# Offsets of two snake convolutions moved ahead of the last product series of a 9x9 convolution

## The chip, the cores and the metric

The kernel runs on one core of a Trainium2 chip. Its time is the time of the device in microseconds (us). A core has a matrix engine (TensorE, in the profile PE for the products and PEld for the loading of their stationary operand), a vector engine (VectorE, DVE), an activation engine (ScalarE, ACT), a general engine (GpSimd, POOL) and a synchronising engine (SyncE, SP). Each takes its own instructions strictly in the order in which the program holds them. Transfers (DMAs) are issued by an engine's queue (SPq and ACTq here) and then run beside the engines. SBUF is the on-chip memory of 128 partitions, PSUM the memory into which TensorE writes.

## The reference, cut to what matters

The kernel computes a sequence of four layers on two images of 128 channels and 64x64 pixels: an attention, a block of three convolutions in parallel, a residual step and a state-space scan in four directions. The change lies in the second layer alone:

```python
h = gelu(affine(conv2d(x, cv1_w, 1), cv1_g, cv1_b))             # stem, 3x3, 64 channels
o0 = silu(affine(conv2d(h, conv0_w, K // 2), conv0_g, conv0_b)) # the 9x9 convolution, 128 channels
ox = dsconv(h, ..., morph=0)                                    # snake along one axis
oy = dsconv(h, ..., morph=1)                                    # and along the other
out = silu(affine(conv2d(concatenate([o0, ox, oy]), fuse_w, 0), fuse_g, fuse_b))

def dsconv(x, ...):
    off = tanh(affine(conv2d(x, off_w, 1) + off_b, off_g, off_beta))  # 18 offsets a pixel
    cum = cumulate_from_center(...)          # running sums of 9 of them, outwards from the middle
    ys = hg + cum                            # (or xs = wg + cum)
    feat = bilinear_sample(x, ys, xs)        # positions are clipped to 0 .. 63
    out = einsum('bkhwc,ock->bohw', feat, w) + b
    return silu(group_norm(out, gn_g, gn_b, out.shape[1] // GN_DIV))
```

The snakes and the 9x9 convolution all read h and nothing of each other. Their three results meet in the 1x1 convolution with fuse_w.

## The kernel before, in words

`layer1` calls three functions one after the other: `stem_and_wide`, `offsets`, `snakes`. All three hold their main work in blocks in which the order of the instructions is the order in which the Python code issues them.

**stem_and_wide** first computes h into the tile `hz` (L560). The 9x9 convolution then runs as a fast algorithm with six combined columns per row (the tiles `comb0` to `comb5`, weights in `w9`), over two halves of the image (k = 0 and 1). For each half there are six series of products, in the order x = 1, 2, 3, 4, 0, 5. A series is 27 pairs of matmuls, one of each pair for each image (L600), into two PSUM tiles. PSUM tiles come from a ring of eight, all with the name m. Behind each series DVE and ACT combine the results (L640 to L661), and `fuse` multiplies finished tiles with the 1x1 weights (L608) and copies them to `xa` (L612 on ACT, L614 on DVE). A finished tile is fused behind the next series, so that the tiles s of series 0 are fused behind series 5, and the tiles q of series 5 at the very end, when nothing is left behind which to hide the silu they wait for.

**offsets** has its own pools. It loads its constants by ACT's queue (L677 to L685), after `layer1` has loaded the snakes' weights on the same queue (L482 to L489). For each of four pairs of row blocks it runs a 3x3 convolution of h (L697, 18 matmuls), a tanh on ACT (L705), the running sums as two matmuls (L709), the adding of the pixel grid on DVE (L711) and four clamps into `yt` (L720), two on DVE and two on POOL. The order is convolution k + 1, then the rest of k. At the end two DMAs on SP's queue store `yt` to the DRAM tensor `pos` (L731).

**snakes** walks over 34 chunks of four lines, 17 for each direction. For a chunk it needs its hats: four DMAs on SP's queue (`positions`, L782) read the positions back from `pos`, spread over 64 partitions each, 256 KB a DMA. ACT then takes the distance of each position from the pixel's index (L791), and DVE clamps it to a triangle (L792). `transposed` turns four lines of h by TensorE (L769) and copies them to `lines` on ACT (L770). `sample` multiplies lines with hats (L809) and copies the result to `feat` (L821, L823), and `convolve` (L835, L846) is run behind every second chunk. The loads run three chunks ahead of the samples and the hats two, in four buffers. Ahead of the loop stand the loads of chunks 0 to 2 and then, for chunks 0 and 1, `transposed` and `hat`.

Of the kernel before, what the change touches and what calls it, by code (L numbers as in the profile page):

```python
# [10 lines left out]
F32 = mybir.dt.float32  # L11
# [4 lines left out]
AF = mybir.ActivationFunctionType  # L16
ALU = mybir.AluOpType
AX = mybir.AxisListType
PSUM = bass.MemoryType.PSUM

P = 128
NB = 2
HW = 64
L = HW * HW
BLK = 512
NBLK = L // BLK
RB = BLK // HW
# [3 lines left out]
KC = K9 // 2  # L31
# [30 lines left out]
def img(t):  # L62
    return t.rearrange("p (r w) -> p r w", w=HW)


def vec(g, name):
    i = VI[name]
    return g.vecs[:, i : i + 1]
# [397 lines left out]
def layer1(g, I):  # L466

    nc, tc = g.nc, g.tc
    with ExitStack() as ctx:
        big = ctx.enter_context(tc.tile_pool(name="l1big", bufs=1))
        hz = big.tile([P, H8, H8], F32, name="hz")
        fw = big.tile([P, 3, P], F32, name="fw")
        nc.scalar.dma_start(fw, I["fuseT"])
        stem_and_wide(g, I, hz, fw)
        pp = ctx.enter_context(tc.tile_pool(name="l1p", bufs=1))  # L480
        grp = pp.tile([P, P], F32, name="grp1")
        nc.scalar.dma_start(grp, I["grp_div"])  # L482

        dsc = pp.tile([P, 2, P], F32, name="dsc")
        dsw = pp.tile([P, 2, KC, P], F32, name="dsw")
        for b in range(2):
            half = slice(64 * b, 64 * b + 64)
            nc.scalar.dma_start(dsc[half], I["dscT"][:, :, KC])
            nc.scalar.dma_start(dsw[half], I["dscT"][:, :, b * (KC + 1) : b * (KC + 1) + KC])  # L489

        dr = ctx.enter_context(tc.tile_pool(name="l1dr", bufs=1, space=bass.MemoryType.DRAM))
        pos = dr.tile([64, L], F32, name="pos")
        offsets(g, I, hz, pos)
        with ExitStack() as bctx:
            snakes(g, bctx, hz, pos, dsc, dsw, grp, fw)


def stem_and_wide(g, I, hz, fw):

# [5 lines left out]
    nc, tc = g.nc, g.tc  # L507
    RP = 32
    NF = HW // 4
    NQ = K9 // 3  # L510
    NX = 6
    CR = RP + KC
    with ExitStack() as ctx:
# [1 line left out]
        ps = ctx.enter_context(tc.tile_pool(name="l1ps", bufs=8, space=PSUM))  # L515

        spdq = [[a.tile([P, BLK], F32, name=f"{n}{b}") for n in "spdq"] for b in range(NB)]
        comb = [a.tile([P, NQ, CR, NF], F32, name=f"comb{i}") for i in range(NX)]

        cw = comb[5].rearrange("p q r i -> p (q r i)")[:, : 9 * 64].rearrange("p (t o) -> p t o", o=64)  # L520
        nc.sync.dma_start(cw, I["cv1T"])
# [94 lines left out]
        with tc.manual_schedule():  # L616
# [10 lines left out]
            ready = []  # L627
            for k in range(HW // RP):
                for x in (1, 2, 3, 4, 0, 5):
                    m = [ps.tile([P, BLK], F32, name="m") for b in range(NB)]  # L630
                    for pair in zip(*(product(m[b], x, b, k) for b in range(NB))):
                        for f in pair:
                            f()
                    for job in ready:
# [30 lines left out]
                fuse(*job)  # L665


def offsets(g, I, hz, pos):

    nc, tc = g.nc, g.tc  # L670
    with ExitStack() as ctx:
        a = ctx.enter_context(tc.tile_pool(name="l1o", bufs=1))
        sm = ctx.enter_context(tc.tile_pool(name="l1osm", bufs=2))
        ps = ctx.enter_context(tc.tile_pool(name="l1ops", bufs=2, space=PSUM))

        ow = a.tile([P, 9, 64], F32, name="ow")
        nc.scalar.dma_start(ow, I["offT"])  # L677
        ov = a.tile([P, 3], F32, name="ov")
        cmat = a.tile([P, 64], F32, name="cmat")
        grid = a.tile([P, NBLK // 2, BLK], F32, name="grid")  # L680
        for e in range(2):
            half = slice(64 * e, 64 * e + 64)
            nc.scalar.dma_start(ov[half], I["offv"])
            nc.scalar.dma_start(cmat[half], I["cum"])
            nc.scalar.dma_start(grid[half], I["grid"].rearrange("p (k e x) -> p k e x", e=2, x=BLK)[:, :, e, :])  # L685
        ob = a.tile([P, 1], F32, name="ob")
        nc.vector.scalar_tensor_tensor(ob, ov[:, 0:1], ov[:, 1:2], ov[:, 2:3], ALU.mult, ALU.add)
        yt = a.tile([64, L], F32, name="yt")

        def conv(k):  # L690
            pc = ps.tile([P, BLK], F32, name="pc")
            for t in range(9):
                dy, dx = divmod(t, 3)
                x0 = KC - 1 + dx
                for e in range(2):
                    y0 = (k + e) * RB + KC - 1 + dy
                    nc.tensor.matmul(  # L697
                        pc[64 * e : 64 * e + 64, :], ow[:, t, :], hz[:, y0 : y0 + RB, x0 : x0 + HW],
                        start=(t == 0), stop=(t == 8),
                    )  # L700
            return pc

        def place(k, pc):
            th = sm.tile([P, BLK], F32, name="th")
            nc.scalar.activation(th, pc, AF.Tanh, bias=ob, scale=ov[:, 0:1])  # L705
            pu = ps.tile([P, BLK], F32, name="pu")
            for e in range(2):
                half = slice(64 * e, 64 * e + 64)
                nc.tensor.matmul(pu[half, :], cmat[half, :], th[half, :], start=True, stop=True)  # L709
            y0 = sm.tile([P, BLK], F32, name="y0")  # L710
            nc.vector.tensor_add(y0, pu, grid[:, k // 2, :])  # L711
            for e in range(2):
                r0 = (k + e) * RB
                for di in range(2):
                    out = img(yt[32 * di : 32 * di + 32])
                    if di == 0:
                        out = out.rearrange("p w h -> p h w")
                    src = img(y0[64 * e + 32 * di : 64 * e + 32 * di + 32])
                    eng = nc.gpsimd if e else nc.vector
                    eng.tensor_scalar(out[:, r0 : r0 + RB, :], src, 0.0, HW - 1.0, ALU.max, ALU.min)  # L720

        with tc.manual_schedule():
            last = None
            for k in range(0, NBLK, 2):
                pc = conv(k)
                if last:
                    place(*last)
                last = (k, pc)
            place(*last)
        for di in range(2):  # L730
            nc.sync.dma_start(pos[32 * di : 32 * di + 32], yt[32 * di : 32 * di + 32])  # L731


def snakes(g, ctx, hz, pos, dsc, dsw, grp, fw):

    nc, tc = g.nc, g.tc
    CN = 4
    NT = KC
    FAR = KC + 1
    NCH = (HW + NT - 1 + CN - 1) // CN  # L740
    RING = 16
    sm = ctx.enter_context(tc.tile_pool(name="l1sm", bufs=2))
    om = ctx.enter_context(tc.tile_pool(name="l1om", bufs=3))
    bp = ctx.enter_context(tc.tile_pool(name="l1b", bufs=1))
    wk = ctx.enter_context(tc.tile_pool(name="l1wk", bufs=4))
    psb = ctx.enter_context(tc.tile_pool(name="l1psb", bufs=2, space=PSUM))
    psf = ctx.enter_context(tc.tile_pool(name="l1psf", bufs=4, space=PSUM))
    psa = ctx.enter_context(tc.tile_pool(name="l1psa", bufs=1, space=PSUM))

    lines = bp.tile([P, RING // CN, CN, 64], F32, name="lines")  # L750

    feat = bp.tile([P, NB, RING, NT, HW], F32, name="feat")
    oraw = bp.tile([P, NB, L], F32, name="oraw")
    hats = {}
# [2 lines left out]

    def transposed(di, n):

        if di > 1 or n >= HW // CN:  # L760
            return
        pt = psb.tile([P, BLK], F32, name="pb")
        v = pt[:, : CN * 64].rearrange("p (i c) -> p i c", c=64)
        for i in range(CN):
            u = n * CN + i + KC
            for b in range(NB):
                half = slice(64 * b, 64 * b + 64)
                line = hz[half, KC : KC + HW, u] if di == 0 else hz[half, u, KC : KC + HW]
                nc.tensor.matmul(v[half, i, :], line, g.ident[half, half], start=True, stop=True)  # L769
        nc.scalar.mul(lines[:, n % (RING // CN)], v, -1.0)  # L770

    def positions(di, m):

        if di > 1:
            return
        hats[di, m] = wk.tile([P, 2, NT, CN, HW], F32, name="hats")
        for b in range(NB):
            for x in range(2):

                o = (32 * di + 9 * b + FAR * x) * L + m * CN * HW  # L780
                src = pos.rearrange("r x -> (r x)")[o : o + NT * (L - HW)].rearrange("(t x) -> t x", x=L - HW)
                nc.sync.dma_start(  # L782
                    hats[di, m][64 * b : 64 * b + 64, x].rearrange("p t i h -> p t (i h)"),
                    src[:, : CN * HW].partition_broadcast(64),
                )

    def hat(di, m):

        if di < 2:
            v = hats[di, m].rearrange("p x t i h -> p (x t i h)")  # L790
            nc.scalar.activation(v, v, AF.Abs, bias=vec(g, "npixel"))  # L791
            nc.vector.tensor_scalar(v, v, 1.0, 0.0, ALU.subtract, ALU.min)  # L792

    def sample(di, m, i):

# [110 lines left out]
        return turns  # L906

    with tc.manual_schedule():
        for n in range(3):
            positions(0, n)  # L910
        for n in range(2):
            transposed(0, n)
            hat(0, n)
        for n in range(2 * NCH):
            di, m = divmod(n, NCH)
            if m == 0:
# [1054 lines left out]
```

## Time and profile before

| what | us |
| --- | --- |
| median of 3 runs (lowest to highest) | 5609.14 (5607.44 to 5610.11) |
| the profiled execution: its time | 5610.11 |
| the profiled execution: its span | 5608.3 |
| start of the first product of the stem (L560) | 1083.1 |
| start of the first product of the 9x9 convolution (L600) | 1146.8 |
| first and last issue of a chunk's load (L782) | 1490.0, 1768.3 |
| first and last start of a sample's product (L809) | 1506.4, 1785.7 |

All times within the kernel count from the start of the profiled span. A line of the timeline or of the chain of waits begins with the start and the duration in us, then comes the engine, then the source line with what it writes and reads, and last, in brackets, how long the engine stood idle before and what it then got. The number behind an x is the number of instructions merged into the line. TensorE makes two passes for a matmul of 32-bit numbers, and the profile counts each: a series of 54 matmuls is x108, a convolution of 18 is x36.

### The profile page before, as it was taken

To read this page: it belongs to the slowest core of one execution; us is meant where nothing else is said; L and a number is where in the kernel's file an instruction comes from. 1 tells how busy PE (TensorE), PEld (TensorE's weight loads), DVE (VectorE), ACT (ScalarE), POOL (GpSimd) and SP (SyncE) were. 2 spreads that over 40 slices of the span, in tenths; PEclk is the share of its full clock that TensorE was granted. 3 is DMA by queue.
4 is the path that set the end of the run, shared out by engine and by line. 5 is a ranking of instruction groups with operands and counts; after the bars stand their busy time and mean duration, and the time that the engine had idled before them with its cause. 6 is when DMAs were issued, how large, how long until landed. Compare 5 with 4: busy or idle time off the path is not lost.

```text
span 5608.3 us, 54471 instructions
## 1 busy us (share of the span) xinstructions
PE 4731.0 (84%) x17062; PEld 1757.8 (31%) x17062; DVE 4537.0 (81%) x4232; ACT 4086.5 (73%) x6282; POOL 3661.7 (65%) x1197
## 2 busy tenths in 40 slices
PE   6999999899788699777788887878888888877786
PEld 3444444344344244222222222222222222222221
DVE  6566555552144998699999999999999999999998
ACT  3999999500255311698888888888888888888886
POOL 6222222100100311599999999999999999999999
PEclk8999999999899899888888888888878787888887
DMA  4111111300375000465565556556555655565554
GB/s 155 38 46 46 31 31 38 62 1 1 76 128 83 27 0 0 104 143 129 129 141 137 135 126 144 129 129 148 140 133 128 144 134 131 130 147 131 134 137 106
DMA packets 334569, 554.27 MB, mean 99 GB/s; under 512 B 69264, under 2 KB 115872, under 8 KB 334080
## 3 DMA queue, kind: packets, MB, share of 16 engines
q1 hardware_dynamic: 331136, 547.17, 41.2%
q10 hardware_dynamic: 3136, 3.56, 0.3%
q8 instruction: 135, 2.21, 0.2%
q14 instruction: 162, 1.33, 0.1%
HBM read 461.40 MB, written 89.13 MB: 98 GB/s over the span
## 4 chain that ended last, share of the span: by engine, by line
DVE 45%; PE 35%; ACT 11%; issue 5%; DMA 2%; POOL 1%; SPq 1%; DVEq 0%; ACTq 0%; POOLq 0%
DVE db L1558 30%; DVE db L1522 11%; PE ps L312 8%; PE acc L328 8%; PE m L1112 5%; PE m L600 5%; ACT da L1544 4%; PE acd L846 2%; ACT db L1550 1%; DVE gt L1585 1%; PE m L560 1%; ACT L1409 1%; ACT u L1409 1%; PE pf L809 1%; DMA hats<-pos 1%
## 5 line engine op out<-in xcount | busy, mean ns | idle before, releaser
L1568 POOL TENSOR_TENSOR db<-db,c 128x2048 f32<-128x2048 f32 x512 | 2314.0, 4535 | 48.3 <-ACT hl L1563 32.7
L1544 ACT ACTIVATE da<-dd,am 128x512 f32<-128x512 f32 x2048 | 1398.6, 687 | 300.4 <-DVE db L1558 281.6
L1558 DVE TENSOR_TENSOR_SCAN db<-da,db 128x512 f32<-128x512 f32 x1376 | 1585.2, 1204 | 36.3 <-ACT db L1550 28.1
L318 ACT ACTIVATE e<-ps 128x1536 f16<-128x1536 f32 (+1 forms) x683 | 919.0, 1624 | 7.9 <-PE ps L312 7.9
L1558 DVE TENSOR_TENSOR_SCAN db<-da,hl,db 128x512 f32<-128x512 f32 x672 | 825.9, 1271 | 41.6 <-POOL db L1531 2.6
L1522 DVE TENSOR_TENSOR db<-pbc,dd 128x2048 f32<-128x2048 f32 (+1 forms) x384 | 781.3, 2035 | 32.1 <-DMA dd<-dx 32.1
L1531 POOL TENSOR_TENSOR db<-b,dd 128x2048 f32<-128x2048 f32 (+1 forms) x192 | 773.5, 4029 | 12.7 <-DMA b<-bx 12.7
L1576 PE MATMUL py<-db,fold 128*32 128x512 f32 x4096 | 615.6, 687 | 153.2 <-POOL db L1568 153.1
L312 PE MATMUL ps<-q 128*128 128x512 f16 x2048 | 554.0, 379 | 4.3 <-DVE flag L260 2.7
L328 PE MATMUL acc<-e,v 128*128 128x512 f16 x2048 | 553.7, 379 | 0.1
L346 POOL TENSOR_TENSOR parts<-parts 32x512 f32<-32x512 f32 x64 | 80.6, 1259 | 707.5 <-DVE parts L345 707.5
L1550 ACT ACTIVATE db<-da,db,hl 128x1 f32<-128x1 f32 x1120 | 394.0, 352 | 146.7 <-DVE db L1522 103.2
L339 DVE RECIPROCAL rec<-acc 32x512 f32<-32x512 f32 x64 | 214.9, 3358 | 257.9 <-PE acc L328 248.3
L1112 PE MATMUL m<-v,u 128*128 128x512 f32 x864 | 379.3, 602 | 41.8 <-DVE v L1055 40.9
L1469 PE MATMUL pm<-dd,ident 128*128 128x512 f32 x512 | 359.7, 841 | 2.5 <-ACT dd L1462 2.5
L1428 PE MATMUL pm<-u,wxp 128*72 128x512 f32 x256 | 196.7, 913 | 141.0 <-ACT u L1409 141.0
L1501 PE MATMUL pbc<-bc,sel 64*128 64x512 f32 x384 | 208.3, 542 | 123.6 <-DVE db L1522 122.8
L312 PEld LDWEIGHTS <-q 128*128 128x128 f16 x2048 | 197.7, 97 | 278.5 <-issue 103.6
L328 PEld LDWEIGHTS <-v 128*128 128x128 bf16 x2048 | 199.3, 97 | 248.8 <-issue 10.2
L600 PE MATMUL m<-comb,w 64*128 64x512 f32 (+4 forms) x1296 | 269.9, 575 | 0.0
L720 POOL TENSOR_SCALAR yt<-y 32x512 f32<-32x512 f32 x8 | 18.1, 2268 | 380.8 <-DVE y L711 380.4
L1576 PEld LDWEIGHTS py<-db,fold 128*32 128x32 f32 x4096 | 90.6, 114 | 553.2 <-issue 306.7
(324 smaller groups left out, 6563.4 us busy)
## 6 DMA issues: line engine op xcount, KB each, us to landing
dd<-dx SPq DMA_DIRECT2D x1024, 256.0 KB, 6.5
dx<-dd SPq DMA_DIRECT2D x128, 512.0 KB, 5.4
c<-bx SPq DMA_DIRECT2D x1024, 64.0 KB, 2.1
hats<-pos SPq DMA_DIRECT2D x136, 256.0 KB, 9.8
b<-bx SPq DMA_DIRECT2D x512, 64.0 KB, 4.6
piece<-qd SPq DMA_DIRECT2D x128, 128.0 KB, 2.8
piece<-kd SPq DMA_DIRECT2D x112, 128.0 KB, 2.7
w<-in_conv0T SPq DMA_DIRECT2D x18, 288.0 KB, 8.5
```

The source lines that it names most:

```text
L312: nc.tensor.matmul(ps[:, i, :], t[:, 1, kb * P : (kb + 1) * P], t[:, 0, qb * BLK : (qb + 1) * BLK], start=True, stop=True,)
L318: nc.scalar.activation(e[:, :n, :], ps[:, :n, :], AF.Exp, scale=1.0 / UP**2)
L328: nc.tensor.matmul(acc, v3[b][:, kb, h, :], e[:, i, :], start=(kb == 0), stop=(kb == NS - 1))
L600: yield lambda q=q, dy=dy, src=src, i0=i0, i1=i1: nc.tensor.matmul(m[:, i0 * NF : i1 * NF], w[half, dy, q, x, :], src, start=(dy == KC and ...
L1112: nc.tensor.matmul(m[x], weights[j][:, dy, x, :], v[j][b][:, x, r0 : r0 + RP, :].rearrange("p r i -> p (r i)"), start=(dy == 0), stop=(dy ...
L1522: nc.vector.tensor_tensor(db_tile(k)[:, :, :n], G[k].pop("pb")[:, :n].unsqueeze(1).to_broadcast([P, 4, n]), S[i]["d4", hf][:, 1, :, :n], A ...
L1531: nc.gpsimd.tensor_tensor(db_tile(k)[:, :, n:], S[i]["b", ng][:, n:].unsqueeze(1).to_broadcast([P, 4, BLK - n]), S[i]["d4", hf][:, 1, :, n ...
L1544: nc.scalar.activation(da, S[i]["d4", hf][:, 0, q, :], AF.Exp, scale=am[:, hf, q, ng : ng + 1])
L1550: nc.scalar.activation(b0, da[:, first : first + 1], AF.Identity, bias=b0, scale=hl[:, hf, ng, q, :])
L1558: nc.vector.tensor_tensor_scan(d1, d0, d1, 0.0 if zero else hl[:, hf, ng, q, :], ALU.mult, ALU.add)
L1568: nc.gpsimd.tensor_mul(v, v, S[i]["c", ng].unsqueeze(1).to_broadcast([P, 4, BLK]))
L1576: nc.tensor.matmul(S[i]["y", hf][32 * q : 32 * q + 32, :], fold, G[k]["db"][:, q, :], start=False, stop=(ng == NNG - 1),)
```

## The change

The function `offsets` and the head of `snakes` become a class `Ahead`, whose parts are called from within the last of the twelve series of products (k = 1, x = 5) of `stem_and_wide`.

- The tiles `comb1` to `comb4` become slices of a tile `early`, allocated for the whole layer. After their last series, `early` holds the snakes' weights, the group matrix, `lines` and the hat buffers of chunks 0 and 1 (`near`). The other two hat buffers (`far`) are allocated in `snakes`, over memory that `stem_and_wide` used.
- `load` is called ahead of series 0. It issues 13 DMAs on SP's queue: constants of the offsets into the parts of `w9` that belonged to series 1 to 4, and the weights of the snakes into `early`. ACT's queue issues none of them any more.
- `convs` is called ahead of series 5: the four 3x3 convolutions, each followed by the rest of the one before it. Their PSUM tiles come from the ring m.
- `beside` is called within series 5. Ahead of pair 2 it issues the rest of the last convolution, the two stores to `pos` and the loads of chunks 0 and 1; ahead of pairs 12 and 15 the turned lines 0 to 3 and 4 to 7; ahead of pair 24 the hat of chunk 0.
- All four clamps of a pair of blocks run on DVE. `yt` lies in eight pieces of 512 numbers, so that the stores to `pos` have rows of 2 KB in place of 16 KB.
- `snakes` begins with the loads of chunk 2 and the hat of chunk 1; its loop is as before.

```diff
-        stem_and_wide(g, I, hz, fw)
...
-        offsets(g, I, hz, pos)
+        early = big.tile([P, 4, 3, HW // 2 + KC, HW // 4], F32, name="early")
...
+        ahead = Ahead(g, I, hz, early, pos)
+        stem_and_wide(g, I, hz, fw, early, ahead)
         with ExitStack() as bctx:
-            snakes(g, bctx, hz, pos, dsc, dsw, grp, fw)
+            snakes(g, bctx, hz, ahead, fw)
...
-        comb = [a.tile([P, NQ, CR, NF], F32, name=f"comb{i}") for i in range(NX)]
+        comb = [early[:, i - 1] if 0 < i < 5 else a.tile([P, NQ, CR, NF], F32, name=f"comb{i}") for i in range(NX)]
...
                 for x in (1, 2, 3, 4, 0, 5):
+                    last = k == HW // RP - 1
+                    if last and x == 0:
+                        ahead.load(w)
+                    if last and x == 5:
+                        ahead.convs(ps)
                     m = [ps.tile([P, BLK], F32, name="m") for b in range(NB)]
-                    for pair in zip(*(product(m[b], x, b, k) for b in range(NB))):
+                    for n, pair in enumerate(zip(*(product(m[b], x, b, k) for b in range(NB)))):
+                        if last and x == 5:
+                            ahead.beside(n, ps)
                         for f in pair:
                             f()
...
+class Ahead:
...
+    def load(self, w):
...
+        dma = g.nc.sync.dma_start
+        c = w.rearrange("p y q x o -> p (y q) (x o)")[:, :, P : 5 * P]
+        self.yt = c[:64, 0:NBLK]
...
+    def convs(self, ps):
+        for k in range(0, NBLK, 2):
+            pc = self.conv(k, ps)
+            if self.placed:
+                self.place(*self.placed, ps)
+            self.placed = k, pc
+
+    def beside(self, n, ps):
+        if n == 2:
+            self.place(*self.placed, ps)
+            for di in range(2):
+                rows = slice(32 * di, 32 * di + 32)
+                self.g.nc.sync.dma_start(self.pos[rows].rearrange("p (c x) -> p c x", c=NBLK), self.yt[rows])
+            for m in range(2):
+                self.positions(0, m, self.near[m])
+        elif n in (12, 15):
+            self.transposed(0, (n - 12) // 3, ps.tile([P, BLK], F32, name="m"))
+        elif n == 24:
+            self.hat(self.near[0])
...
-                    eng = nc.gpsimd if e else nc.vector
-                    eng.tensor_scalar(out[:, r0 : r0 + RB, :], src, 0.0, HW - 1.0, ALU.max, ALU.min)
+                nc.vector.tensor_scalar(out, src, 0.0, HW - 1.0, ALU.max, ALU.min)
...
     with tc.manual_schedule():
-        for n in range(3):
-            positions(0, n)
-        for n in range(2):
-            transposed(0, n)
-            hat(0, n)
+        for m in range(2):
+            hats[0, m] = slots[m]
+        positions(0, 2)
+        hat(0, 1)
         for n in range(2 * NCH):
```

## The prediction, on record before the changed kernel ran

> **What bounds the kernel now.** The page gives no bound for this change: its shares are means over four layers. I read the chain of waits from 1395 to 1530 us, cut to its longer pieces (start, duration, what):
>
> ```profile
> 1404.86 22.57 PE m L600 x108
> 1427.44 1.93 PE m L608 x4
> ...
> 1431.11 2.00 PE m L608 x4
> ...
> 1436.41 4.92 DMA ow<-in_offT
> ...
> 1441.46 17.55 PE pc L697 x72
> ...
> 1460.02 7.94 PE pc L697 x36
> ...
> 1468.96 7.94 PE pc L697 x36
> 1476.91 1.03 PE pu L709 x4
> ...
> 1483.68 2.35 POOL yt L720
> 1486.04 3.93 DMA pos<-yt
> ...
> 1507.26 10.07 DMA hats<-pos
> 1517.36 2.00 ACT hats L791
> ```
>
> The last series, the offsets and the loading of the first positions stand one behind the other. TensorE carries it to 1478, POOL's clamps to 1486, then transfers to 1517. Next the timeline of ACT for the hats of chunks 0 to 4; the bracket is ACT's idle time and what ended it:
>
> ```profile
> 1503.04 2.00 ACT L791 ACTIVATE hats<-hats,vecs 128x2048 f32<-128x2048 f32 x1 [9.87 <-DMA hats<-pos]
> 1511.07 2.00 ACT L791 ACTIVATE hats<-hats,vecs 128x2048 f32<-128x2048 f32 x1 [5.76 <-DMA hats<-pos]
> 1517.36 2.00 ACT L791 ACTIVATE hats<-hats,vecs 128x2048 f32<-128x2048 f32 x1 [3.25 <-DMA hats<-pos]
> 1524.11 2.00 ACT L791 ACTIVATE hats<-hats,vecs 128x2048 f32<-128x2048 f32 x1 [3.52 <-DMA hats<-pos]
> 1531.36 2.00 ACT L791 ACTIVATE hats<-hats,vecs 128x2048 f32<-128x2048 f32 x1 [4.01 <-DMA hats<-pos]
> ```
>
> Every hat waits for its load, at some 7 us a chunk. The table by stretches (span, PE busy and instructions, clock, DMA share, GB/s) shows why:
>
> ```profile
> 1494.00:1506.00 12.00, 0.45 (x8) 0.50 0.84 150
> ```
>
> The DMA engines are 84% busy at 150 GB/s while TensorE stands still. So the snakes' start is paced by loads, and what counts is when the loads of chunks 0, 1 and above all 2 are issued.
>
> **The change, step by step, against the profiled execution (5610.11 us, span 5608.3).** Everything up to 1404.86, the start of series 5, keeps its place: same products, and the tiles `w9` and `comb5` keep their addresses.
>
> *Loads of constants.* Before, ACT issued twelve after its last copy (1433.42 to 1440.8), and the first convolution waited 8.37 us for `ow`, to 1441.46. Now SP issues thirteen when series 4 ends, about 1404.86 - 3.7 (four fusings) - 22.6 = 1378.6. SP holds nothing else there: its wait before the first store (L731) is the rest of the stage. At 0.6 us an issue they are out by 1387 and the first two have 26 us for a landing that took 4.92. Cost zero, covered by series 0; without that cover 5 us. DVE's small `ob` (0.22 us) now stands ahead of series 0's results, and waits for two of these loads; DVE is idle there until 1402.
>
> *Convolutions on TensorE.* 4 x 7.94 + 3 x 1.02 (running sums) = 34.8, so series 5 starts at 1404.86 + 34.8 = 1439.7. I take 7.94 for all four: the first two took 17.55 before, 1.67 above 2 x 7.94, behind the idle time that is now gone. A tanh takes 0.78 and hides behind the next convolution, as before. Silu and tanh need no table load between them in the trace. The ring m is safe: each PSUM tile's last reader is at least one convolution old.
>
> *Series 5 with its guests.* 22.57 + 1.02 (last sums) + 2 x 1.10 (turned lines; 32 took 2.19) = 25.8: it ends at 1465.5, and the fusing of s at 1467.4.
>
> *The positions.* Two pairs in (2 x 22.57/27 = 1.7) and 1.0 for the sums: 1442.4. The adding 0.77, then three DVE clamps at 0.62 until direction 0 is whole: 1445.0. POOL's 9.2 us of clamps leave the path, and nothing is left on POOL's queue. The store landed in 3.93; for rows of 2 KB and a second store beside it I add 0.5 (between 0 and 1.7, since a pair of 512 KB loads into `gt` took 5.6): 1449.4. Chunk 0's hat began 13.05 us behind its first load's issue (1489.99 to 1503.04): 1462.5. Chunk 1's took 21.1, but with chunk 2 already loading. Here chunk 2 cannot, so the bound from below is 2.1 MB at 150 GB/s, 14 us, plus 1. I take 16, nearer to that since the competitor is missing: 1465.4.
>
> *The new wait.* In the built order the hat of chunk 1 stands on ACT and DVE **ahead of** what follows series 5: the copies of s, the adding to q (L658), its silu, the copies of q. So TensorE's last two fusings, ready at 1467.4, wait for chunk 1's load. Hat on ACT 1465.4 to 1467.4, on DVE to 1468.7, a copy 0.92, q starts at 1469.6; before, from q's start (1429.45) to the end of its fusing (1433.11) it took 3.66: 1473.3. Queued behind are the third group of turned lines and every sample. Worse, the buffer of chunk 2 lies over q of image 1, and its first DMA waits on SP for this last fusing, with all later loads behind it. So the transfers stand still from about 1465 to 1474.
>
> *A rule against it.* The trace has fused q behind 1.76 us of idle TensorE at full speed (2.00 us). Now the gap is 1467.4 to about 1471.5, over 4 us. The Trainium skill ("TensorE: Matmul & The Clock Gate", part 1) states that an idle window of about 3.4 us halves the clock and a busy one of equal length restores it. By the row the fusing costs 2.0, by the rule 4.0: the sum loses 0 or 2. The trace's own case is the first convolution behind 8.37 us; 4 us lies just over the rule's window, which runs freely. I take 1: the last fusing ends at **1474.3**.
>
> *Sum.* Chunk 2's loads are issued at 1474.3 into idle DMA engines, as chunk 0's were at 1489.99, so its hat begins 13.05 later, at 1487.35 against 1517.36: **30.0 us** earlier. Chunk 4, with the spacing of a start (8.03 + 6.29), comes at 1501.7 against 1531.36: 29.7. The samples agree: chunk 0's could start behind the turned lines at 1475.5 against 1506.40, 30.9. Behind that, loads and samples both stand 30 us earlier with the same work, so the rest of the layer moves along. At the layer's end the loads of `gt` now wait for a late silu (about 1826 in old time) in place of the hats (1785.98); they landed in 5.6 and DVE needs them at 1839.25, so 7 us cover is left, cost zero. 5610.1 - 30.0 = 5580.1; the profiled execution is 1 us above the median of the runs, so I predict **5579**.
>
> **Rivals.**
>
> *The wait for chunk 1 is as long as before* (20%). If its load takes the old 21.1 us, its hat starts at 1470.5 and all that follows comes 5.1 later; with 2 us of slow clock the gain is 24: 5585. For it: the old spacing of 8.03 between the first two hats. Against: that was with a third chunk in flight.
>
> *The new wait is short* (20%). Chunk 1 lands with chunk 0, its hat follows that at 1464.5 and the clock stays: 0.9 + 1 more, and 0.5 for the store, so 32.5: 5577. Loads in flight together share the engines and could end together, which speaks for it.
>
> *The gain is partly given back later* (6%, half of it within 0.2% of no change). Between 1650 and 1735 ACT hardly waits for loads any more; samples and group norm pace it, with spells of half clock. If the spells fall worse, up to some 20 us go: 5600.
>
> *Slower: the loads' pace* (3%). In the built order the 136 loads have 91 waits on TensorE where they had 30: each DMA of a chunk waits for its own last product, and one that waits holds up SP's queue behind it. If this lengthens a chunk from 7.05 us by more than 30/34 = 0.9, the change loses; at 1.2 us the time is 5610 - 30 + 34 x 1.2 = 5621. Against it: the products waited for are those of four chunks back, as before, and SP's waits on L809 summed to only 8.4 us up to 1600.
>
> **How the numbers follow.** The forecast has 51% (gain 27 to 32). Worst of its terms: a store at 5.6 (-1.2), slow clamps at 1.2 each (-1.7), chunk 1 late (-5.1), cold clock (-1): a gain of 21, time 5588. Best: 32.5, and some 4 us for other spells of slow clock, 5573. The range 5573 to 5588 covers forecast and first two rivals less their tails. About 0.2%, 11 us, is what a measurement tells from no change. Faster by more: 51 + 20 + 20 + 3 = 94%; within: 3%; slower: 3%.
>
> **What would show it.** In the changed profile: no gap ahead of the convolutions, their first two in 16 us; series 5 from about 35 us later than its fellow; the store issued near 1445, chunk 0's hat near 1462.5; a TensorE gap behind the fusing of s that ends with DVE's q; the load of chunk 2 issued right behind the last fusing, near 1474; chunks from 2 on 30 us earlier, and the same 30 at the first product of the next layer (1852.92). A hat of chunk 1 at 1470 would prove the first rival, a spacing of chunks over 8 us the last. The prediction is wrong if the convolutions wait for their constants, or if the 30 us at chunk 2 do not arrive at 1852.92.

## The result, and the profile after

| | before | after |
| --- | --- | --- |
| median of the runs, us (lowest to highest) | 5608.39 (5606.01 to 5610.11, 6 runs) | 5576.92 (5574.42 to 5579.26, 6 runs) |
| the profiled execution: time, span | 5610.11, 5608.3 | 5576.86, 5574.9 |
| first issue of a chunk's load | 1489.99 | 1450.07 |
| chunk 2's hat begins | 1517.36 | 1491.01 |
| first product of the next layer | 1852.92 | 1822.05 |

The changed kernel is faster by 31.5 us: ratio 0.9944, 95% interval 0.9931 to 0.9957. The forecast was 5579, a gain of 30.0, in a range of 5573 to 5588.

The chain of waits of the changed kernel, from 1395 to 1510 us, cut to the pieces that answer to those shown of the kernel before (start, duration, what):

```profile
1405.66 15.74 PE m L728 x72
...
1422.41 7.94 PE m L728 x36
...
1431.36 7.94 PE m L728 x36
...
1440.30 1.92 PE m L590 x8
1442.22 1.03 PE m L741 x4
...
1445.66 4.39 DMA pos<-w
...
1459.24 9.23 DMA early<-pos
...
1468.58 2.01 ACT early L802
...
1470.61 1.23 DVE early L803
1471.84 0.97 DVE xa L604
1472.81 0.53 DVE q L655
...
1473.36 0.82 ACT q L658
...
1474.23 3.80 PE m L598 x4
...
1487.15 11.10 DMA hats<-pos
...
1498.35 2.00 ACT hats L802
```

The convolutions (L728) stand where series 5 began, with no wait for their constants. Series 5 (L590) is on the chain for two pairs only; the store is issued at 1445.66, where it was issued at 1486.04. Then the chain runs through something that was not on it before: the load of chunk 1, its hat on ACT and DVE (L802, L803), and only behind these, on the same two engines, what the last fusing (L598) needs. That fusing takes 3.80 us, where it took 2.00. Chunk 2's load is issued right behind it, at 1478.04, and chunk 3's behind that; the transfer and the hat shown last are chunk 3's.

The timeline of ACT, hats of chunks 0 to 4 with the silu of q between them:

```profile
1463.52 2.00 ACT L802 ACTIVATE early<-early,vecs 128x2048 f32<-128x2048 f32 x1 [6.33 <-DMA early<-pos]
1468.58 2.00 ACT L802 ACTIVATE early<-early,vecs 128x2048 f32<-128x2048 f32 x1 [3.06 <-DMA early<-pos]
1473.36 1.52 ACT L658 ACTIVATE q<-q,vecs 128x512 f32<-128x512 f32 x2 [1.80 <-DVE q L655]
1491.01 2.00 ACT L802 ACTIVATE hats<-hats,vecs 128x2048 f32<-128x2048 f32 x1 [7.80 <-DMA hats<-pos]
1498.35 2.00 ACT L802 ACTIVATE hats<-hats,vecs 128x2048 f32<-128x2048 f32 x1 [4.11 <-DMA hats<-pos]
1506.03 2.00 ACT L802 ACTIVATE early<-early,vecs 128x2048 f32<-128x2048 f32 x1 [4.44 <-DMA early<-pos]
```

Against 1503.04, 1511.07, 1517.36, 1524.11 and 1531.36 the five hats are 39.5, 42.5, 26.3, 25.8 and 25.3 us earlier. 16 us of what chunk 1 won are lost again before chunk 2. The table by stretches (span, then busy time of PE, PEld, DVE, ACT and POOL with their instructions, the clock, the DMA share, GB/s) says where:

```profile
1450.00:1462.00 12.00, 12.00 (x80) 6.36 (x78) 0.00 (x0) 0.77 (x2) 0.00 (x0) 1.00 0.85 139
1470.00:1478.00 8.00, 3.77 (x4) 1.18 (x4) 4.38 (x5) 3.08 (x4) 0.00 (x0) 0.72 0.00 0
1478.00:1490.00 12.00, 7.13 (x113) 6.49 (x112) 1.11 (x4) 2.42 (x6) 0.00 (x0) 0.76 0.73 106
```

In the first line TensorE is busy throughout and the DMA engines 85% of the time, which is what the change does. In the second the DMA engines carry nothing for 8 us, although 15 of the first snake's 17 chunks are still to be loaded.

The changed kernel's execution stands 0.8 us later than that before when the convolutions begin (1405.60 for 1404.79). From that common point chunk 2's hat is 27.2 us earlier, and the next layer 31.7. The kernel before was traced once; another kernel with its order of work (four fixed tiles, below) needed 2.0 us more for the same stretch, so the 27.2 is no better known than that.

### The profile page after: what moved, and what is told of

It reads as the page before. It is cut to its first block, busy times and chain, and to the rows that moved or that the text cites. A ratio compares the mean times of both kernels' runs of the same rounds, so it can differ in the third digit from the quotient of the medians.

```text
span 5574.9 us, 54509 instructions
## 1 busy us (share of the span) xinstructions
PE 4717.5 (85%) x17062; PEld 1756.9 (32%) x17062; DVE 4540.1 (81%) x4240; ACT 4087.5 (73%) x6282; POOL 3642.2 (65%) x1189
## 4 chain that ended last, share of the span: by engine, by line
DVE 43%; PE 35%; ACT 10%; issue 6%; DMA 2%; POOL 2%; SPq 1%; DVEq 0%; POOLq 0%; ACTq 0%
DVE db L1607 29%; DVE db L1571 10%; PE ps L312 8%; PE acc L328 8%; PE m L1161 6%; PE m L590 4%; ACT da L1593 4%; PE acd L896 2%; ACT db L1599 1%; DVE gt L1634 1%; PE m L550 1%; ACT L1458 1%; ACT u L1458 1%; PE pf L859 1%; POOL db L1617 1%
## 5 line engine op out<-in xcount | busy, mean ns | idle before, releaser
L1571 DVE TENSOR_TENSOR db<-pbc,dd 128x2048 f32<-128x2048 f32 (+1 forms) x384 | 780.7, 2033 | 31.5 <-PE pbc L1550 31.5
L1625 PE MATMUL py<-db,fold 128*32 128x512 f32 x4096 | 602.7, 674 | 153.9 <-POOL db L1617 153.7
L1453 PE MATMUL pm<-xn,wcs 128*128 128x512 f32 x512 | 235.3, 603 | 17.0 <-ACT xa L1652 10.5
```

What stands on the lines that cost most here:

```text
L1571: nc.vector.tensor_tensor(db_tile(k)[:, :, :n], G[k].pop("pb")[:, :n].unsqueeze(1).to_broadcast([P, 4, n]), S[i]["d4", hf][:, 1, :, :n], A ...
L1625: nc.tensor.matmul(S[i]["y", hf][32 * q : 32 * q + 32, :], fold, G[k]["db"][:, q, :], start=False, stop=(ng == NNG - 1),)
```

## The experiments

Each is given with its edit, what was expected, and what it measured. Medians stand beside the runs of the kernel before on the same chip.

### The convolutions back behind the last series

Everything else of the change stays: constants loaded ahead, clamps on DVE, buffers as in the changed kernel.

```diff
-                    if last and x == 5:
-                        ahead.convs(ps)
...
-                        if last and x == 5:
-                            ahead.beside(n, ps)
...
             for job in ready:
                 fuse(*job)
+            ahead.convs(ps)
+            for n in (2, 12, 15, 24):
+                ahead.beside(n, ps)
```

> The changed kernel with the four convolutions, the stores, the first loads and the first hat behind the last series in place of inside it; loads of constants, clamps on DVE and buffers as changed. Theory (the gain is the chain from the last series to chunk 2's load, made shorter in two ways): what is left is the 8.4 us wait for the constants, the 1.7 us of slow clock behind it and about 3.9 us of POOL's clamps, 14 us in all: 5595. Rival (laying the offsets beside the series gives nothing, since TensorE has the same products to do; all comes from the loads and clamps): 5577. Rival (the loads and clamps give nothing, all comes from the overlap): 5608.

Measured: 5593.29 us (8 runs) for 5610.02 before; ratio 0.9973, 0.9962 to 0.9984. Its timeline of TensorE, around the last fusing:

```profile
1430.02 1.98 PE L598 MATMUL m<-q,fw 128*128 128x512 f32 x4 [1.76 <-ACT q L654]
1431.93 15.80 PE L727 MATMUL m<-hz,w 128*64 128x512 f32 x72
```

The first convolutions follow the fusing at once, and two take 15.80, where two took 17.55 behind 8.37 us of idle time. The store is issued 41.9 us behind the start of the last fusing (1430.02 to 1471.94), in the kernel before 54.9 (1431.11 to 1486.04). So 13.0 of the change's gain have nothing to do with the overlap that gives it its name. In the medians 16.7 of 31.5 stay without it, close to the 14 expected; its own chunk 2 is 12.3 earlier, counted from the last fusing, and most of the rest comes later (see the sum below).

### Only the clamps, in the kernel before

```diff
-                    eng = nc.gpsimd if e else nc.vector
+                    eng = nc.vector
```

> The kernel before, with all sixteen clamps of the offsets on VectorE, none on GpSimd. It prices one part of the change by itself. Theory: the store of the positions waits for GpSimd's last two clamps, so it is issued some 3.9 us earlier than in the kernel before (1486.04 us from the span's start, at the same start of the offsets), and every hat of the first snake moves with it by 3.5 to 4.3; the time falls to about 5605 to 5607 where the kernel before stands at 5610. Rival: the clamps on GpSimd were hidden and all of the 13.1 to 13.5 us that the offsets gained when they stayed behind the ninth series came from the constants loaded ahead; then nothing moves by more than 1 us.

Measured: 5604.34 us (one run) for 5607.20. The end of the offsets on DVE:

```profile
1479.60 0.69 DVE L711 TENSOR_TENSOR y<-pu,grid 128x512 f32<-128x512 f32 x1 [6.12 <-PE pu L709]
1480.32 2.05 DVE L720 TENSOR_SCALAR yt<-y 32x512 f32<-32x512 f32 x4
1482.40 0.69 DVE L711 TENSOR_TENSOR y<-pu,grid 128x512 f32<-128x512 f32 x1
1483.13 2.11 DVE L720 TENSOR_SCALAR yt<-y 32x512 f32<-32x512 f32 x4
```

One time within the spread of the kernel before (5604.21 to 5611.47) proves nothing, so the trace has to say it. From the last fusing to the store it is now 52.2 us (1432.64 to 1484.86) for 54.9: the clamps on POOL cost **2.7**, not 3.9, mostly because the last adding (no bracket) now waits in DVE's own queue behind the third pair's clamps and starts 49.8 us behind the fusing, for 48.9. Of the 13.0, the remaining 10.3 are put down to the constants: the wait of 8.37 and the 1.75 by which the convolutions behind it were slow make 10.1.

### Chunk 1's hat behind the first samples

```diff
-        hat(0, 1)
         for n in range(2 * NCH):
...
                 sample(di, m, i)
+            if n == 0:
+                hat(0, 1)
```

> The changed kernel with the hat of chunk 1 issued behind the samples of chunk 0, so that neither ACT nor DVE waits for chunk 1's load ahead of the last q. Theory (that wait holds the last fusing, and so the load of chunk 2): the gap of TensorE ahead of the last fusing falls from 5.6 to below 2 us, the fusing runs at full clock (2.0 us for 3.8), chunk 2's load is issued about 5.6 us earlier (1472.4 for 1478.04) and the kernel ends as much earlier: 5571. Rival (the loads' rate alone sets the start, the wait is hidden under it): no change, 5577.

Measured: 5574.17 (4 runs) for 5610.02; ratio 0.9935, 0.9918 to 0.9951. Its fusings on TensorE, and below those of the changed kernel:

```profile
1468.25 1.98 PE L598 MATMUL m<-s,fw 128*128 128x512 f32 x4
1471.99 1.98 PE L598 MATMUL m<-q,fw 128*128 128x512 f32 x4 [1.76 <-ACT q L658]
```

```profile
1466.63 1.98 PE L598 MATMUL m<-s,fw 128*128 128x512 f32 x4
1474.23 3.78 PE L598 MATMUL m<-q,fw 128*128 128x512 f32 x4 [5.62 <-ACT q L658]
```

The gap falls from 5.62 to 1.76 us, the fusing runs at full clock, and chunk 2's load is issued 5.75 us behind the start of the fusing of s for 11.41. So ACT and DVE did hold the fusing of q behind a hat that has nothing to do with it, since their instructions run in the order of the program. From the start of the fusing of s to the next layer's first product this kernel needs 352.2 us and the changed one 355.4: of the 5.7, 3.2 reach the end of the layer, so the time lies between the two expected. The intervals of the two kernels' ratios overlap, so the trace carries this verdict, not the time.

### Chunk 2's buffer away from q

My prediction gave the overlap of this buffer with q as the reason why chunk 2's load waits. Here the two `far` tiles are allocated last, so that in the built program they lie wholly within the 9x9 weights, whose last readers are done when series 5 is.

```diff
-    far = [ahead.as_hats(bp.tile([P, 2 * NT * CN * HW], F32, name=f"hats{i}")) for i in range(2)]
-    slots = ahead.near + far
     feat = bp.tile([P, NB, RING, NT, HW], F32, name="feat")
     oraw = bp.tile([P, NB, L], F32, name="oraw")
+    far = [ahead.as_hats(bp.tile([P, 2 * NT * CN * HW], F32, name=f"hats{i}")) for i in range(2)]
+    slots = ahead.near + far
```

> The changed kernel with the two far hat buffers behind feat and oraw in memory, so that they lie over the 9x9 weights and not over q; the hat of chunk 1 stays ahead of q. Theory: chunk 2's load follows chunk 1's without a gap (issue near 1461.7 for 1478.04), but it now takes bandwidth from chunk 1, whose hat moves from 1468.6 to about 1471.2 and holds the last fusing 2.6 us longer; chunk 2 is ready when its samples come, at about 1489 for 1494.4: 5 us gained, 5572. Rival (loads pace the whole first snake): all 13 us that chunk 2's hat comes earlier are gained: 5564. Rival (chunk 1's delay decides): 2.6 us lost, 5580.

> Both edits together: hat of chunk 1 behind the samples of chunk 0, far buffers over the 9x9 weights. Theory: neither wait is left, samples of chunk 0 start near 1474.5 for 1480.1, those of chunk 2 near 1483 for 1494.4: 11 us gained, 5566. Rival (one of the two edits alone takes all there is to gain): the better of the two single edits, 5571.

The second has the hat moved as well. Measured: 5581.71 and 5574.84 (4 runs each) for 5610.02; ratios 0.9948 (0.9931 to 0.9964) and 0.9936 (0.9919 to 0.9952). The edit moved the tiles and did nothing else that was meant. The queue of SP in the first of the two:

```profile
1451.29 12.04 SPq L794 DMA_DIRECT2D early<-pos  x8
1479.79 11.95 SPq L794 DMA_DIRECT2D hats<-pos  x8
```

The fusing of q ends in that execution at 1479.76, and chunk 2's first load is still issued right behind it: SP had waited 16.4 us for that fusing, in the changed kernel 16.3, and in both built programs the load waits for the same count of TensorE's products. The addresses are not what it waits for. With the hat moved it is issued at 1473.99, as without this edit. My theory fell here. That the first of the two is some 5 us slower than the changed kernel stays open: 3.9 of it lie between the fusing of s and the next layer, and its interval overlaps the changed kernel's.

### One tile that outlives the convolution

The next theory: a tile opened in a scope that begins when another closes waits for that whole scope. So the 9x9 weights go into a tile `late` that lives as long as the layer, and the buffers of chunks 2 and 3 into its part whose last readers are series 5's first products.

```diff
+        late = big.tile([P, K9 * (K9 // 3) * 6 * P], F32, name="late")
...
-        w = a.tile([P, K9, NQ, NX, P], F32, name="w9")
+        w = ahead.late.rearrange("p (y q x o) -> p y q x o", y=K9, q=NQ, x=NX)
...
-    far = [ahead.as_hats(bp.tile([P, 2 * NT * CN * HW], F32, name=f"hats{i}")) for i in range(2)]
+    far = [ahead.as_hats(ahead.late[:, lo + i * n : lo + (i + 1) * n]) for i in range(2)]
```

(`feat` and one half of `oraw` move into `late` as well; `lo` is 9216 and `n` 2048.)

> The changed kernel, with the 9x9 weights, and after them the hats of chunks 2 and 3, the sampled lines and one half of the raw outputs, in one tile that outlives the convolution, so that chunk 2's load no longer waits for the release of everything that the convolution held, but only for series 5's first products. Theory: the loads of chunks 0 to 3 then follow one another from 1450 us without the gap of 16 us (1461.6 to 1478.0) in which nothing was loaded; chunk 2's hat comes by 1483 to 1486 instead of 1491.0, its products at about 1487 instead of 1494.4, the products bound the pace from there, and the time falls by 4 to 8 us against the changed kernel, to about 5569 to 5573. Against it stands that chunk 1's hat, which is queued ahead of the last fusing, comes later the more loads share the queues: if at about 1475 instead of 1468.6, the fusing and all behind it lose what the load gains. Rival: loads and products have the same pace of 7.4 us a chunk and an earlier load only waits longer for its products; then 5575 to 5579.

> As the kernel with the one long-lived tile, and chunk 1's hat queued behind the first chunk's products, so that the last fusing waits for no load. Theory: chunk 2's products at about 1485.5 us from the start instead of 1490.3 with the hat moved alone; 4 to 5 us less than that kernel, about 5568 to 5570 where before stands at 5610. Rival: the loads' start decides nothing any more, as the products pace the chunks; then 5573 to 5575, as with the hat moved alone.

Measured: 5562.99 and 5558.37 (4 runs each) for 5607.20; ratios 0.9921 (0.9904 to 0.9937) and **0.9912** (0.9896 to 0.9929). The queue of SP, first with the one tile alone, then with the hat moved too:

```profile
1445.29 11.57 SPq L795 DMA_DIRECT2D early<-pos  x8
1456.96 13.65 SPq L795 DMA_DIRECT2D late<-pos  x8
1478.91 11.85 SPq L795 DMA_DIRECT2D early<-pos  x8
```

```profile
1444.97 11.58 SPq L795 DMA_DIRECT2D early<-pos  x8
1456.65 13.89 SPq L795 DMA_DIRECT2D late<-pos  x8
1470.68 13.85 SPq L795 DMA_DIRECT2D early<-pos  x8
```

Chunk 2's load now follows chunk 1's without a gap, and with the hat moved the queue stays full through chunk 5. The hat of chunk 2 begins 17.6 and 11.6 us behind the start of the fusing of s, for 24.4 in the changed kernel. The first kernel also shows the cost that was set against it. Its last fusing:

```profile
1472.02 3.44 PE L599 MATMUL m<-q,fw 128*128 128x512 f32 x4 [8.22 <-ACT q L659]
```

With chunk 2's transfers in the same queues, chunk 1's hat comes 21.1 us behind chunk 0's first issue (1445.29 to 1466.37), and the gap grows from 5.62 to 8.22. The hat moved behind the samples ends that: 1.76 again.

Both times are well under what was expected, and the traces say why, by what their brackets show ahead of the convolution: the start of the stem had moved too. The first products of the stem, in the changed kernel and in the one with the long tile:

```profile
1083.48 64.16 PE L550 MATMUL m<-xa,comb 128*64 128x512 f32 x288 [7.92 <-DMA comb<-in_cv1T]
```

```profile
1079.23 63.61 PE L551 MATMUL m<-xa,comb 128*64 128x512 f32 x288 [2.19 <-DMA comb<-in_cv1T]
```

### What moved the stem

> The changed kernel, with the loads of the 9x9 convolution's weights held back until the stem's own weights have landed (a copy of 18 columns that reads the one and writes the other). It takes apart the gain of the kernel with the one long-lived tile, in whose trace the stem began 4.2 us earlier (1079.23 us for 1083.48), after 2.19 us of waiting for its weights instead of 7.92, because there the 9x9 weights' loads were issued 12 us later. Theory: that part of the gain has nothing to do with the offsets; held back here, the stem begins by 1078 to 1080, the ninth series still begins with no gap, all behind it comes 4 to 6 us earlier, and the time is 4 to 6 us under the changed kernel's, 5571 to 5573. Rival: the earlier stem was only where that execution stood, within the 2 us by which starts differ; then the time is the changed kernel's within 2 us, and the whole 14 us of the long-lived tile are the chunk loads'.

> The changed kernel itself, unaltered, on the chip and in the call of the kernel with the weights held back, so that the two stand against the same runs of the kernel before: 5574 to 5579, and the stem's products beginning 1 to 2 us about 1083.5.

The edit of the first, ahead of the loads of the 9x9 weights:

```diff
+        nc.vector.tensor_copy(
+            w[:, 0::3, 0, :, 0], cw[:, 0, 0:18].rearrange("p (y x) -> p y x", x=NX)
+        )
```

Measured: 5579.98 and 5578.39 (4 runs each) for 5608.80; ratios 0.9949 (0.9933 to 0.9966) and 0.9949 (0.9932 to 0.9965). The weights' loads were issued 7 us later, and the stem waited as long as before:

```profile
1085.68 64.14 PE L553 MATMUL m<-xa,comb 128*64 128x512 f32 x288 [7.98 <-DMA comb<-in_cv1T]
```

So holding the 9x9 weights back gains nothing. It does not show that other transfers never slow the stem's load, for another one came up into their place, the 2 MB transfer to `xs`. SP's queue in this kernel, then in the changed one and in the one with the long tile:

```profile
1078.62 0.36 SPq L511 DMA_DIRECT2D comb<-in_cv1T  x1
1079.04 0.55 SPq L523 DMA_DIRECT2D xs<-xa  x1
```

```profile
1076.49 0.36 SPq L511 DMA_DIRECT2D comb<-in_cv1T  x1
```

```profile
1074.94 0.36 SPq L512 DMA_DIRECT2D comb<-in_cv1T  x1
```

What differs is the issue of the stem's own load: 1076.49 in the changed kernel, 3.0 us behind the start of the last attention product (1073.49), but 1074.94 with the long tile, at that product's start (1074.97), and there 2.9 us ahead of SP's next transfer, where the changed kernel has 0.4. In the built order this load waits for the release of the whole layer before in the one, and for a few named instructions in the other. It also lands in 4.3 us for 7.0; whether because it is issued ahead of the rest, no run here takes apart.

To divide the gain, the buffers of chunks 2 and 3 went back into the snakes' pool, with the long tile otherwise kept:

```diff
-    far = [ahead.as_hats(ahead.late[:, lo + i * n : lo + (i + 1) * n]) for i in range(2)]
+    far = [ahead.as_hats(bp.tile([P, 2 * NT * CN * HW], F32, name=f"hats{i}")) for i in range(2)]
```

> The changed kernel with the 9x9 weights, and after them the sampled lines and the raw outputs, in the one long-lived tile, but the buffers of chunks 2 and 3 in the snakes' own pool, so that chunk 2's load waits for the convolution's release as in the changed kernel. It divides the 14 us of the kernel with the long-lived tile into what the chunk loads bring and what the layout brings ahead of the stem. Theory: the stem begins 4 to 5 us earlier, as there (waiting about 2 us for its weights, not 8), chunk 2's load is issued behind the last fusing and its hat comes some 22 us behind the fusing of s, 24.4 in the changed kernel, 17.6 in that with the long tile; the time is 5571 to 5574. Rival: the earlier stem was that execution's; then 5576 to 5579, and the chunk loads bring all 14.

Measured: 5570.22 (4 runs) for 5608.58; ratio 0.9934, 0.9917 to 0.995. The stem waits 2.81 us, and chunk 2's hat begins 24.8 us behind the fusing of s. Time from the start of that fusing to the next layer's first product, in each trace:

| kernel | us |
| --- | --- |
| changed kernel, both executions | 355.4, 355.6 |
| long tile, chunk 2 in the snakes' pool | 355.1 |
| hat of chunk 1 moved | 352.2 |
| chunk 2 away from q; the same, and the hat moved | 359.3; 351.9 |
| long tile, with chunk 2 in it | 344.5 |
| the same, and the hat moved | 340.9 |

So chunk 2's early load is worth 10.6 to 10.9 us in this stretch, with the hat moved 14.5, and the stem's early start some 5.5 ahead of it (the last attention product to the stem: 8.7 to 11.0 us in the ten traces without the long tile, 4.3 to 4.9 in the three with it). Over the whole program 38.4 us are gained by the layout with the change, 44.2 with chunk 2 in the tile and 48.8 with the hat moved. By these medians the early load is worth 5.8 and with the hat moved 10.4, less than the traces say: the traced execution of the long tile is the fastest of its four (5560.97), that of the layout alone the slowest (5571.60). **The last is the best kernel found.**

### The waits of each transfer, in the kernel before

Of the changed kernel's lead of 30.9 us at the next layer, 4.5 had come behind chunk 2, in a stretch that the change hardly touches. This was one candidate:

```diff
-    wk = ctx.enter_context(tc.tile_pool(name="l1wk", bufs=4))
+    slots = [bp.tile([P, 2, NT, CN, HW], F32, name=f"hats{i}") for i in range(4)]
...
-        hats[di, m] = wk.tile([P, 2, NT, CN, HW], F32, name="hats")
+        hats[di, m] = slots[(di * NCH + m) % 4]
```

> The kernel before, with the four buffers of hats as four fixed tiles in place of a rotating pool of four. Only the waits of the loads differ: each of a chunk's four transfers waits for the products that read its own part of the buffer, where before the first transfer waited for all of them. It is to say where the late gain of the changed kernel comes from, the 4.5 us between chunk 2 (26.3 us earlier than before) and the next layer's first product (30.9 earlier). Theory: the finer waits bring it; then the chunks of the first snake stand within 1 us of the kernel before, the last two chunks and the next layer's first product come 2 to 4.5 us earlier, and the time is 5604 to 5608 where before stands at 5610. Rival: it comes from elsewhere (the granted clock, the tiles' places); then the next layer's first product stands within 1 us of before's.

Measured: 5608.05 (12 runs) for 5607.20; ratio 0.9999, 0.999 to 1.0008. The finer waits show no gain, though the interval alone would just admit one of 4.5 us. The stretch from chunk 2's hat to the next layer takes 330.9 us here, 330.3 in the kernel with the clamps alone, which has the old waits, 331.0 and 331.2 in the changed kernel, 326.9 to 333.8 in the others, and 335.6 in the one execution of the kernel before. That last is the long one of the set, so the late gain is mostly that execution's own, as far as one trace can tell, and not the change's.

## Why the prediction was right, and where its steps were off

The mechanism came as predicted: the offsets run under series 5, the load of chunk 1 becomes a new wait ahead of the last fusing, and chunk 2's load waits for that fusing. Two terms were mis-sized and one reason was wrong.

**Constants, convolutions, series 5.** As predicted: no gap, 15.81 us for the first two convolutions, the store issued at 1445.66 for 1445.8 (1445.0 and the later start of 0.8). Four clamps took 2.07 to 2.10 us, 0.5 each where 0.62 was taken. Series 5 with its guests took 26.4 for 25.8. The store landed in 4.39 (4.4), chunk 0's hat came 13.45 behind its load's issue (13.05).

**Chunk 1's load** is the first mis-sized term: 16 us from chunk 0's first issue to chunk 1's hat, measured 18.5. That is half way to the old 21.1; 2.1 MB at the 139 GB/s of that stretch take 15 us, to which the start of the first transfers comes. With chunk 2's load behind it, in the kernel with the long tile, it was 21.1 again, so the prediction's reason, the missing competitor, held, and its worth was taken too high. Neither of the first two rivals, 21.1 and a hat right behind chunk 0's, came true.

**The clock** is the second: between the row's 2.0 and the rule's 4.0 I took 3.0, and the fusing took 3.78, at a granted clock of 0.50 throughout. The gap was 5.62 us, not just over 4, since chunk 1 came late, so the case that I weighed was not the one that ran. Six executions with gaps of 5.35 to 8.22 us show 3.44 to 3.78 for the fusing, at a granted clock of 0.50 to 0.57; those with 1.76 show 1.98, at 1.00. For these gaps the rule of the Trainium skill ("TensorE: Matmul & The Clock Gate", part 1), that an idle window of some 3.4 us halves the clock, was the better guide. It does not hold to the tenth, and there the measurement decides: behind a gap of 3.05 us, under that window, the first sample products of chunk 1 in three traces got 0.57 to 0.63, from 1.00 before it.

**The wait of chunk 2's load** was placed rightly, behind the last fusing, but its reason was wrong. The prediction put it down to q's address; it is the release of the whole scope, since moving the buffer away from q left the wait (1479.79, behind a fusing that ended at 1479.76), and taking it out of the scope removed it (1456.96, behind chunk 1's load).

**The sum.** Chunk 2's hat came 12.97 us behind its load's issue (13.05). With 2.4 us for chunk 1 and a little under 1 for the clock its lead is 27.2 and not 30.0 from the common start. That the total came out at 31.5 all the same is in part luck. Between the two traced executions 4.5 us come from chunk 2's hat to the next layer and 2.6 behind that, two stretches that the prediction put at nothing; 0.8 are lost ahead of the convolutions, which makes 33.4 with rounding. The 4.5 are mostly the one long execution of the kernel before. The 2.6 recur: from the next layer's first product to the end of the span the ten executions traced here of kernels with the class `Ahead` take 3752.4 to 3754.3 us, the three without it 3754.9 to 3756.2. Which part of the change does this, no run shows. The traced execution of the kernel before stands 1.7 over its median, which leaves 31.5. Nothing of the lead was given back: the sign asked for, chunk 2's gain at the next layer, came (31.7 for 27.2 from the common start), and the loads' pace did not lengthen, with chunks 4 to 14 issued 7.2 us apart.

**The gain's halves.** The prediction counted constants, clamps and overlap into one sum and did not say what each is worth. At the store, 10.3 us are constants loaded earlier, 2.7 clamps, and the rest the overlap: 14.9 at chunk 2 (27.2, less the 12.3 that the kernel with the convolutions behind has there from its own start).

## What to carry to other kernels

When work is moved under another stage, look at what stands between the moved part and the next stage: here a hat queued ahead of a fusing, and a scope's release, cost 14.5 us to the end of the layer in the traces, 10.4 in the medians. A transfer that should run ahead across two stages needed a tile that outlives both; a change of addresses alone did not free it. And before a gain is put down to the overlap that a change is named for, run the change without it: nearly half of this one's lead at chunk 2, 12.3 of 27.2 us, was constants that were fetched late and clamps on POOL.

## What the runs showed of the hardware

- SP's issue of one 256 KB load took 0.6 to 0.8 us for the first four of a burst and 1.7 to 2.5 for the next ones: the eight issues of chunks 0 and 1 took 11.5 to 12.0 us in all ten traces of kernels with the class `Ahead`. From 1490 to 1590 us of the changed kernel it is not this that sets the pace: TensorE is 95% busy there, the DMA engines 80%, 89% of the chain of waits lies on TensorE, and SP waits 35 us for TensorE's products.
- A TensorE gap of 1.76 us left the next four passes at 1.98 us and a granted clock of 1.00; gaps of 5.35 us and more made them 3.44 to 3.78, at 0.50 to 0.57. In between, also from 1.00: a gap of 1.84 was followed by 1.00 and one of 1.83 by 0.92, one of 2.59 by 0.84, and three of 3.05 by 0.57 to 0.63.
- The stem's load of 0.3 MB landed in 4.3 and 4.9 us where it was issued 3 us ahead of the next transfers on SP's and ACT's queues, and in 7.0 and 7.1 where it was issued together with them.
